# A scan whose two sweeps multiply the state itself instead of its two summands

## The chip, the cores and the metric

One core of a Trainium2 chip runs the whole program. The metric is device time in microseconds (us). The engines are TensorE (PE; its weight loads are listed as PEld), VectorE (DVE), ScalarE (ACT), GpSimd (POOL) and SyncE (SP), which issues most DMAs. Three runs of the kernel before took 1889.16, 1890.15 and 1891.19 us.

## The reference

The input is one sequence of 4096 rows of 512 values, and a context of 3202 rows. All is float32.

```python
x = residual + _mha(layernorm(x), layernorm(ctx), W_qkv, b_qkv, W_o, b_o)   # 8 heads of 64
U = (layernorm(x) @ W_in.T + b_in) @ Bmat                                   # 4096 x 64

def step(s, u_t):
    s = silu(s @ A.T) + u_t
    return (s, s)
_, states = scan(step, zeros(64), U)                                        # 4096 steps in a row
x = x + states @ Cmat + mod
```

The change touches the scan alone: a chain of 4096 steps, each a product with a 64x64 matrix, a silu and an addition.

## The kernel before, in words

**Attention.** The queries are cut into 8 blocks Q of 512, and each block into units (Q, hp, half): a pair of heads hp and half of the block's queries. A unit goes through 13 key chunks; for each, PE makes `s` (L1144), ACT takes the exponential to `p` (L1222), PE makes the product `po` (L1280), and DVE adds `p` up in `acc` (L1230). When a unit is through, PE sums `acc` over the partitions into two banks `pd` (L1309), ACT copies them to `rd` (L1353), DVE takes the reciprocal (L1358), the sum of it (L1361) and scales the unit's output `o` (L1369). The last unit of all, (7, 3, 1), has one tile `pd_last` instead of these banks. For the last 256 queries, the projections `yb` (L2112) take all four head pairs of block 7: `o_7_0_1` holds pairs 0 and 1, `o_7_2_1` pairs 2 and 3.

**The scan.** The 4096 steps are cut into 256 chunks of L = 16 steps. 128 chunks lie in the free dimension and two halves of 64 states in the partitions, so that one step of all chunks is one operation on a 128x128 tile. The tile `u` holds 2U. Sweep "a" (`sweep` at L1971, tiles `za`) starts every chunk at zero. Its last states, `end1`, moved on by one chunk, start sweep "b" (tiles `z`), whose states are the result; the end of b is compared with the end of a, and if anything differs by more than TOL a general and slow path runs. That path doesn't run here.

A step needs z, the product of the matrix with the state. The state is h + u, where h = (1 + tanh(z/2)) z. The kernel before never multiplies the sum. `terms` (L1962) multiplies four steps of `u` at once into a PSUM bank of 4 x 128 columns, ahead of the steps, and `z_` (L1984) adds the product with h to a quarter of that bank. So the chain of a step is: PE `z` (L1960), ACT tanh (L1988), DVE h (L1995), PE `z` again. The state itself is made beside the chain, in sweep b alone, by POOL (L2027, two tiles). `products` (L2034) multiplies it with C into 512 columns for each half. Of its two results, one is added to the row by DVE (L2054); the other, for two steps in three, is copied by ACT (L2048) and added by POOL (L2051), and for the third by DVE. Rows of odd steps have both results in `pd_last`, rows of even steps in `py_n` and `py_o`.

The last 256 rows go through layer norm and a scan of their own (`l.*`: L2133 to L2177, tiles `zl`) with warm-up steps, while sweep b runs.

**Order.** All this is recorded by a planner (`Plan`, L76). Each piece has an engine, a cost, the pieces it waits for, tiles of rings that it takes and gives back, and a due time; `SHIFT` (L94) moves the due time of each sort of piece. An engine takes the ready piece that is due first, and the order that comes out is fixed in the program. Two things matter below. Sweep a takes both tiles of the ring "m" when it opens, and gives them back with its last h; the sums `pd` of a unit need the same two tiles. And `PORT` (L92) names the DVE pieces that the planner keeps apart from POOL's.

The tail also holds dummy products: `idle_` (L2241) multiplies a constant 128x128 tile six times after the last step of b. The comparisons (`largest`, `differ`, L2070 to L2084) take the largest state, times TOL, the difference, its absolute value (on ACT), a comparison of each element and a count.

Of the kernel before, what the change touches and what calls it, by code (L numbers as in the profile page):

```python
# [13 lines left out]
AF = mybir.ActivationFunctionType  # L14
# [6 lines left out]
P = 128  # L21
# [14 lines left out]
WARM = 17  # L36
# [4 lines left out]
NCK = T // L // 2  # L41
NP = 11
# [33 lines left out]
class Plan:  # L76
# [18 lines left out]
        "row.store": 2.25, "fold": 21, "rows.outs": -27.25, "heads": 29.5, "spread": 4.5, "query.flip": -21,  # L95
        "states": 3.25, "inverse": 13.25, "extra": 54.75, "scale": -26, "rest": -11.5, "row.mod": -26.25,
        "joined0": 23.25, "b": -0.75, "add.l": -43.5, "l.stats": -74.25, "last": -0.25, "base": -119.25,
        "inverse.l": 12, "rows.inputs": 7, "maximum": -21, "fall": -14.75, "query.stats": 25, "den": -41.5,
        "row.scaled": -22.75, "l.h": 9.25, "row.stats": -52.75, "rows.turn": 10.25, "query.scaled": -65,
        "l.mod": 24.75, "close": -30, "swap": 32, "products": -9.75, "gather.l": -2.75, "l.ys": 51.5,  # L100
        "fall.l": -46.25, "weights": -14, "rows.s": -6.5, "l.x1": 12.25, "l.kept": 1.5, "tq": 37.5,
        "l.store": 35, "row.move3": -73, "l.from": 2.5, "l.copy": -22.75, "l.states": -42.5, "l.turn": -27.25,
        "row.flip": -51, "swap.l": -30.75, "l.near": -25.75, "differ": 2.25, "row.load": 38, "add": 3.25,
        "rest.l": -23, "den.l": -33, "query.factors": 32, "sevenths": 5, "l.z": -5.75, "scale.l": 64.25,
        "outs": 1.5, "output": -59, "query.move3": 10, "number": -8.75, "l.inputs": -15, "q": -3.75,
        "sums": -35, "row.move2": -22.25, "row.move1": 18.25, "query.move0": 62.75, "stored1": -5.5,
        "counted": -14.25, "to": -30.75, "sums.l": -14.75, "row.kept": 17.75, "so": 19, "stored0": 28.25,
        "l.scaled": 3.5, "row.move0": 0.25, "rise": -31.75, "join": -29.5, "sample": -0.5, "l.idle": -22.75,
        "risen": -59.75, "c2": 7.5, "yb": -16, "query.load": 55.25, "query.move2": 13.75, "row.row": -53.75,
        "added": -31.75, "l.terms": -17.75, "joined1": -4.75, "rows.first": -84.5, "sq": -29.75,  # L110
        "row.x1": 30.75, "join.l": 99.75, "start": 18.5, "sevenths.read": -15.75, "product": 0.5,
        "row.factors": -40, "fold.l": 20, "output.l": 47, "table": -34.75, "gather": 18, "outs.read": -15,
        "copied": 0.5, "open": -6.25, "row.copy": 48.5, "l.out": 31.75, "l.factors": -10.25, "a": 32.5,
        "query.move1": 5.25, "fetch": 19.75, "py1": 22.75,
# [118 lines left out]
def xattn_ssm_kernel(  # L233
# [1663 lines left out]
    A_PACE, B_PACE = 1500, 1900  # L1897
# [33 lines left out]
    def open_scan():  # L1931
# [15 lines left out]
        for name, n in (  # L1947
            ("end0", NCK + 1), ("end1", NCK + 1), ("ul", PRE + 1 + P), ("hw", P), ("hl", P),
            ("sl", P + 1), ("df", NCK), ("st", P // LT),
            ("top", 1), ("bad", 1), ("badl", 1), ("badr", 1),  # L1950
        ):
            sv[name] = two[:, at_ : at_ + n]
            at_ += n
# [8 lines left out]
    def terms(z, q, start):  # L1962

        if q:
            on_a(z, u[:, 4 * q - 1 : 4 * q + 3, :], start=True)
            return
        if start is not None:
            on_a(z[:, 0, :], start, start=True)
        on_a(z[:, 1:, :], u[:, :3, :], start=start is None)

    def sweep(k, start, end, d=0, pace=0, after=()):  # L1971

        def bank(q):
            return sv["za" if k == "a" else "z"][q % 2]

        def at_(j):
            return bank(j // 4)[:, j % 4, :]

        def terms_(q):
            terms(bank(q), q, None if start is None else sv[start][:, :NCK])

        def z_(j):  # L1984
            on_a(at_(j), sv["h"][(j - 1) % 3], start=False)

        def tanh_(j):
            nc.scalar.activation(sv["th"][j % 2], at_(j), AF.Tanh, scale=0.5)  # L1988

        def h_(j):  # L1990
            h = sv["h"][j % 3]
            if j == 0 and start is None:
                nc.vector.memset(h, 0.0)
                return
            nc.vector.scalar_tensor_tensor(  # L1995
                h, sv["th"][j % 2], 1.0, at_(j), ALU.add, ALU.mult
            )

        def last_():
            e = sv[end]  # L2000
            nc.vector.tensor_tensor(e[:, 1:], sv["h"][(L - 1) % 3], u[:, L - 1, :], ALU.add)
            nc.vector.tensor_copy(e[NS:, 0:1], e[:NS, NCK : NCK + 1])

        for j in range(L):
            q = j // 4
            if j % 4 == 0:

                free = [(k, "h", 4 * q - 5)] if q > 1 else list(after)
# [693 lines left out]
```

## Time and profile before

| what | us |
|---|---|
| median of three runs | 1890.15 |
| the profiled execution's own time | 1889.67 |
| its span, first to last instruction | 1887.9 |
| what lies around the span | 1.77 |
| PE busy in it | 1873.1 |
| first product of sweep a | 1782.89 |
| first product of sweep b | 1843.93 |
| last DVE instruction of the main program | 1883.88 |

All times inside the program below are counted from the start of the span. In a timeline row stand the start, the length (from the first start to the last end, where several instructions are drawn together), the engine, the line, the operation, output<-inputs, their number, and in brackets how long the engine was idle before and what ended that. In a row of the groups stand the line, the engine, the operation, the shapes, the number, the busy time in us and the mean of one in ns, and the idle time before them.

### The profile page before, as it was taken

The page shows a single profiled execution, that of the slowest core. Times are in us where ns is not written, and L with a number is a line of the kernel's source. Part 1 is how long each engine was busy: PE and PEld are TensorE (multiplying, and loading weights), DVE is VectorE, ACT ScalarE, POOL GpSimd, SP SyncE. Part 2 cuts the span into 40 slices and gives each one's busy share as a digit, 9 for nine tenths or more (in the row PEclk, how much of TensorE's full clock was granted, in tenths as well). Part 3 has the DMA queues.
Part 4 walks back from the last instruction along what each step waited for, and adds up shares of the span by engine and source line. Part 5 has one row for each costly group of instructions (what it writes and reads, how often), then busy time and mean ns, then how long its engine had stood idle before and what let it go on. Part 6 is the DMA issues. An engine that isn't in the chain of part 4 may idle for free.

```text
span 1887.9 us, 69209 instructions
## 1 busy us (share of the span) xinstructions
PE 1873.1 (99%) x29856; PEld 1414.9 (75%) x29856; DVE 1563.3 (83%) x2142; ACT 1166.6 (62%) x1663; POOL 258.2 (14%) x386
## 2 busy tenths in 40 slices
PE   9999999999999999999999999999999999999997
PEld 5887689777777777797777777777777777777684
DVE  6642699788988889798978898898979897989776
ACT  3242577665766577565756676757757575757653
POOL 6120300022000210022002200021002200110105
PEclk9999999999999999999999999999999999999999
DMA  8554133133323333233313332324313331536477
GB/s 257 158 159 120 54 102 92 38 115 90 106 74 105 86 112 97 65 95 111 98 44 108 87 114 79 106 79 117 98 55 98 107 104 44 171 108 182 139 190 238
DMA packets 260770, 207.58 MB, mean 110 GB/s; under 512 B 94632, under 2 KB 233896, under 8 KB 260460
## 3 DMA queue, kind: packets, MB, share of 16 engines
q1 hardware_dynamic: 256440, 196.48, 36.1%
q10 hardware_dynamic: 4020, 6.62, 1.2%
q8 instruction: 237, 3.88, 0.8%
q14 instruction: 73, 0.60, 0.1%
HBM read 156.32 MB, written 29.88 MB: 99 GB/s over the span
## 4 chain that ended last, share of the span: by engine, by line
PE 97%; DVE 1%; ACT 1%; DMA 0%; issue 0%; POOL 0%; SPq 0%; DVEq 0%; ACTq 0%; POOLq 0%
PE po L1280 37%; PE s L1144 36%; PE pax L404 3%; PE qx L404 3%; PE qy L404 2%; PE pay L404 2%; PE pkx L404 2%; PE pvx L404 2%; PE pvy L404 1%; PE pky L404 1%; PE pk L722 1%; PE pv L599 1%; PE pd L1309 1%; PE sm L1164 1%; PE po L1268 1%; PE pu L1747 1%
## 5 line engine op out<-in xcount | busy, mean ns | idle before, releaser
L1222 ACT ACTIVATE p<-s,shifts 128x1024 f32<-128x1024 f32 (+1 forms) x832 | 891.4, 1081 | 418.3 <-PE s L1144 392.7
L1230 DVE TENSOR_TENSOR acc<-p,acc 128x1024 f32<-128x1024 f32 (+1 forms) x704 | 851.0, 1214 | 96.8 <-ACT p L1222 77.2
L1144 PE MATMUL s<-q,k 64*64 64x256 f32 x12800 | 850.6, 376 | 0.2 <-ACT p L1222 0.2
L1280 PE MATMUL po<-p,v 64*64 64x256 f32 x12800 | 848.2, 376 | 1.0 <-DVE o L1335 0.9
L1144 PEld LDWEIGHTS s<-q,k 64*64 64x64 f32 x12800 | 518.9, 133 | 175.2 <-ACT p L1222 13.5
L1280 PEld LDWEIGHTS po<-p,v 64*64 64x64 f32 x12800 | 519.9, 133 | 163.1 <-issue 3.5
L1634 POOL TENSOR_TENSOR xr<-xr,rowb 128x512 f32<-128x512 f32 x28 | 35.7, 1274 | 797.6 <-DVE acc L1230 688.9
L1358 DVE RECIPROCAL rd<-rd 128x256 f32<-128x256 f32 (+1 forms) x64 | 110.0, 1719 | 6.4 <-ACT rd L1353 6.4
L1249 ACT COPY swap<-acc 64x256 f32<-64x256 f32 x126 | 50.8, 403 | 64.9 <-DVE acc L1237 61.8
L1230 DVE TENSOR_TENSOR acc<-p,p 128x1024 f32<-128x1024 f32 x64 | 78.2, 1222 | 11.6 <-ACT p L1222 11.5
L1729 POOL TENSOR_TENSOR xr<-x,modb 128x512 f32<-128x512 f32 x28 | 41.6, 1496 | 253.3 <-DVE acc L1254 178.3
L1420 POOL TENSOR_SCALAR rstd_x<-mv_x 128x1 f32<-128x1 f32 x28 | 18.6, 666 | 276.7 <-DVE mv_x L1417 276.0
L1215 DVE TENSOR_TENSOR acc<-x,acc 2x256 f32<-2x256 f32 x128 | 54.9, 429 | 1.5
L1254 DVE TENSOR_TENSOR acc<-swap,acc 64x256 f32<-64x256 f32 x126 | 52.4, 416 | 2.9 <-ACT swap L1249 1.3
L1570 ACT ACTIVATE q<-qx,bias 128x256 f32<-128x256 f32 x42 | 17.6, 470 | 48.0 <-PE qx L404 48.0
L582 DVE TENSOR_TENSOR ks<-pky,ks 128x512 f32<-128x512 f32 x15 | 10.4, 692 | 43.2 <-PE pky L404 23.7
L576 ACT ACTIVATE ks<-pkx,bias 128x256 f32<-128x256 f32 x40 | 16.8, 470 | 44.4 <-PE pkx L404 32.9
L1237 DVE TENSOR_TENSOR acc<-acc 128x512 f32<-128x512 f32 x63 | 43.1, 684 | 0.3
L1335 DVE TENSOR_TENSOR o<-po,o 128x256 f32<-128x256 f32 x64 | 27.0, 423 | 14.1 <-ACT o L1331 13.5
L481 DVE STREAM_TRANSPOSE x<-xh_y 128x512 f32<-128x512 f32 x28 | 18.2, 688 | 21.7 <-ACT xh_y L1428 14.7
L1353 ACT ACTIVATE rd<-pd 128x128 f32<-128x128 f32 x126 | 34.0, 275 | 1.0 <-PE pd L1309 0.4
L1178 DVE TENSOR_REDUCE m<-sm 128x1 f32<-128x256 f32 x64 | 24.0, 417 | 11.3 <-PE sm L1164 11.3
(314 smaller groups left out, 1760.7 us busy)
## 6 DMA issues: line engine op xcount, KB each, us to landing
k<-kd SPq DMA_DIRECT2D x432, 128.0 KB, 2.2
v<-vd SPq DMA_DIRECT2D x432, 128.0 KB, 2.2
xn<-x SPq DMA_DIRECT2D x448, 32.0 KB, 1.9
xr<-in_x_dram SPq DMA_DIRECT2D x30, 256.0 KB, 3.2
x1d<-xr SPq DMA_DIRECT2D x30, 256.0 KB, 2.2
x<-in_x_dram SPq DMA_DIRECT2D x28, 256.0 KB, 3.0
cx<-in_ctx_dram SPq DMA_DIRECT2D x25, 256.0 KB, 4.2
kd<-ks SPq DMA_DIRECT2D x20, 256.0 KB, 2.3
```

The costliest lines, as they stand in the source:

```text
L404: nc.tensor.matmul(to[:, b, :], still[:, i, b * P : (b + 1) * P], moving[:, i, :], start=(start and b == 0 and i == 0), stop=(i == 1), ski ...
L1144: nc.tensor.matmul(s[k0 : k0 + HD, a, b, :], kts[(*w["at"][:2], c)][r, b * CK + k0 : b * CK + k0 + HD], q[r], start=True, stop=True, skip_ ...
L1215: made = nc.vector.tensor_tensor(to[r], t[r], to[r], ALU.add)
L1222: nc.scalar.activation(t[:, :, :nb, :], w["ps"][c][:, :, :nb, :], AF.Exp, bias=w["shift"])
L1230: return nc.vector.tensor_tensor(w["acc"][:, :, :nb, :], t[:, :, :nb, :], before[:, :, :nb, :], ALU.add)
L1237: return nc.vector.tensor_tensor(acc[:, :, 0, :], acc[:, :, 0, :], acc[:, :, 1, :], ALU.add)
L1249: nc.scalar.copy(w["swap"][r], of[(1 - k) * HD : (2 - k) * HD])
L1254: made = nc.vector.tensor_tensor(of[r], w["swap"][r], of[r], ALU.add)
L1280: nc.tensor.matmul(w["po"][k][a * HD : (a + 1) * HD, :QU], vts[Q, hp, c][r, b, a * HD : (a + 1) * HD], t[r, a, b, :], start=(c == 0 and b ...
L1358: nc.vector.reciprocal(w["rd"][:, part], (w["pd"] if last else w["rd"])[:, part])
L1634: return nc.gpsimd.tensor_tensor(xs[half][:, t], xs[half][:, t], rowb, ALU.add)
L1729: return nc.gpsimd.tensor_tensor(xt[:, t], x1[:, t], modb, ALU.add)
```

## The change

1. `terms` is gone. Both sweeps make h as before, then DVE adds `u` to it (a new piece "s", L1980 of the changed kernel) into one of five tiles (NST), and `z_` multiplies that state. PE's sixteen products of `u` (eight in each sweep) go; DVE gets 15 additions in sweep a and 16 in sweep b, less the one in `last_` of each sweep, which becomes a copy.
2. POOL's sixteen additions of sweep b go, since the state is there already. The new piece is not in `PORT`.
3. The six dummy products go.
4. A comparison is now one DVE piece: largest state times TOL, difference, largest absolute difference, comparison of one column. ACT's Abs goes.
5. B_PACE goes from 1900 to 1600, and nearly every number of `SHIFT` is another.

```diff
-WARM = 17
+NST = 5
...
-        "row.store": 2.25, "fold": 21, "rows.outs": -27.25, "heads": 29.5, "spread": 4.5, "query.flip": -21,
+        "row.store": -5.25, "fold": 15.25, "rows.outs": 0.25, "heads": 5, "spread": 4, "query.flip": 3.75,
...
-    A_PACE, B_PACE = 1500, 1900
+    A_PACE, B_PACE = 1500, 1600
...
-        sv["th"] = [one[:, i, :] for i in range(2)]
-        sv["h"] = [one[:, 2 + i, :] for i in range(3)]
-        sv["s"] = [one[:, 5 + i, :] for i in range(2)]
-        sv["ok"] = one[:, 7, :]
+        sv["th"], sv["h"], sv["ok"] = (one[:, i, :] for i in range(3))
+        sv["s"] = [one[:, 3 + i, :] for i in range(NST)]
...
-    def terms(z, q, start):
-
-        if q:
-            on_a(z, u[:, 4 * q - 1 : 4 * q + 3, :], start=True)
-            return
-        if start is not None:
-            on_a(z[:, 0, :], start, start=True)
-        on_a(z[:, 1:, :], u[:, :3, :], start=start is None)
...
+        def state(j):
+            if j < 0:
+                return sv[start][:, :NCK]
+            return sv["s"][j % NST] if j or start is not None else u[:, 0, :]
 
         def z_(j):
-            on_a(at_(j), sv["h"][(j - 1) % 3], start=False)
+            on_a(at_(j), state(j - 1), start=True)
...
+        def state_(j):
+            nc.vector.tensor_tensor(state(j), sv["h"], u[:, j, :], ALU.add)
 
         def last_():
             e = sv[end]
-            nc.vector.tensor_tensor(e[:, 1:], sv["h"][(L - 1) % 3], u[:, L - 1, :], ALU.add)
+            nc.vector.tensor_copy(e[:, 1:], state(L - 1))
...
+        first = 1 if start is None else 0
+        for j in range(first, L):
+            free = [(k, "s", j - 1)] if j > first else list(after)
+            yield (k, "z", j), "PE", 250, partial(z_, j), free, d, [], [], "quarters"
+            yield (k, "tanh", j), "ACT", 240, partial(tanh_, j), [(k, "z", j)], d + 400
+            gives = [("m", "open")] if k == "a" and j == L - 1 else []
+            yield (k, "h", j), "DVE", 210, partial(h_, j), [(k, "tanh", j)], d + 800, [], gives
+            old = [("products", j - NST, part) for part in range(2)] if first == 0 and j >= NST else []
+            yield (k, "s", j), "DVE", 210, partial(state_, j), [(k, "h", j)] + old, d + 800
             d += pace
-        yield (k, "end"), "DVE", 450, last_, [(k, "h", L - 1)], d
-
-    def states(j, h):
-        s = sv["s"][j % 2]
-        nc.gpsimd.tensor_tensor(s, h, u[:, j, :], ALU.add)
-        return s
+        yield (k, "end"), "DVE", 350, last_, [(k, "s", L - 1)], d
...
         nc.vector.tensor_tensor(df, new, old, ALU.subtract)
-        yield
-        nc.scalar.activation(df, df, AF.Abs)
-        yield
-        nc.vector.tensor_scalar(ok, df, top, None, ALU.is_le)
-        nc.vector.tensor_reduce(bad, ok, AX.X, ALU.add)
+        nc.vector.tensor_reduce(far, df, AX.X, ALU.max, apply_absolute_value=True)
+        nc.vector.tensor_tensor(bad, far, top, ALU.is_le)
...
-        def idle_():
-            for k in range(2):
-                nc.tensor.matmul(sv["z"][1][:, k, :], a_t, a_t, start=True, stop=True)
...
-            plan.add(("states", j), "POOL", 450, lambda j=j: states(j, sv["h"][j % 3]),
-                     [("b", "h", j)] + ([("products", j - 2, part) for part in range(2)] if j > 1 else []), e)
```

What the planner makes of it. Up to the middle of unit (7, 0, 1), PE's rows are the same one by one. Further on they differ at three places that the prediction speaks of.

PE, from the last attention products on, before. The rows are the last two products of unit (7, 3, 1), its sums `pd_last`, the projections `yb`, and the start of sweep b (`z`).

```order
L1280 MATMUL po0_7_3_1_24264<-p_7_3_1_12_24439,v_7_3_1_12_24251 64x256
L1280 MATMUL po1_7_3_1_24265<-p_7_3_1_12_24439,v_7_3_1_12_24251 64x256
L1296 MATMUL pd_last_24534<-acc_7_3_1_24175,ones_70 64x256 x4
L2112 MATMUL yb_0_24450<-wo_97,o_7_0_1_23457 128x512
L2112 MATMUL yb_1_24451<-wo_97,o_7_0_1_23457 128x512
L2112 MATMUL yb_0_24450<-wo_97,o_7_0_1_23457 128x512
L2112 MATMUL yb_1_24451<-wo_97,o_7_0_1_23457 128x512
L2112 MATMUL yb_0_24450<-wo_97,o_7_2_1_24229 128x512 x2
L2112 MATMUL yb_1_24451<-wo_97,o_7_2_1_24229 128x512 x2
L1960 MATMUL z_24522<-scan_21420,a_t_91 64x128 x2
L1960 MATMUL z_24522<-u_63,a_t_91 64x384 x2
L1960 MATMUL z_24522<-u_63,a_t_91 64x512 x2
```

The same place now, from the fifteenth and last product of sweep a (`za_1`) on, which stands right behind the last product of unit (7, 3, 1); `pd_7_1_1` and `pd_7_2_1` are the sums of the two units before the last.

```order
L1958 MATMUL za_1_23801<-scan_21420,a_t_91 64x128 x2
L1309 MATMUL pd_7_1_1_0_24525<-acc_7_1_1_23367,ones_70 64x128
L1309 MATMUL pd_7_1_1_1_24526<-acc_7_1_1_23367,ones_70 64x128
L1309 MATMUL pd_7_1_1_0_24525<-acc_7_1_1_23367,ones_70 64x128
L1309 MATMUL pd_7_1_1_1_24526<-acc_7_1_1_23367,ones_70 64x128
L1958 MATMUL z_24420<-scan_21420,a_t_91 64x128 x2
L1309 MATMUL pd_7_2_1_0_24541<-acc_7_2_1_23808,ones_70 64x128
L1309 MATMUL pd_7_2_1_1_24542<-acc_7_2_1_23808,ones_70 64x128
L1309 MATMUL pd_7_2_1_0_24541<-acc_7_2_1_23808,ones_70 64x128
L1309 MATMUL pd_7_2_1_1_24542<-acc_7_2_1_23808,ones_70 64x128
L2078 MATMUL yb_0_24551<-wo_97,o_7_0_1_23463 128x512
L2078 MATMUL yb_1_24552<-wo_97,o_7_0_1_23463 128x512
```

Sweep a now ends behind the attention's products; before, its last `z` stood ahead of `s` of chunk 7 of this unit, with six more `s` and the `po` of ten chunks still to come; so the sums that need its two tiles came behind it too, and the first product of sweep b came between them, ahead of the projections. The row that follows is the second `z`, and two more `yb` pairs come behind it.

DVE at the same place, before: reciprocals and scalings of units (7, 2, 1) and (7, 3, 1). Those of unit (7, 1, 1) stand further ahead, between additions to `acc`.

```order
L1358 RECIPROCAL rd_7_2_1_24427<-rd_7_2_1_24427 128x128
L1369 TENSOR_TENSOR o_7_2_1_24229<-o_7_2_1_24229,rd_7_2_1_24427 128x128
L1361 TENSOR_REDUCE rises_90<-rd_7_2_1_24427 128x1
L1369 TENSOR_TENSOR o_7_2_1_24229<-o_7_2_1_24229,rd_7_2_1_24427 128x128
L1335 TENSOR_TENSOR o_7_2_1_24229<-po1_7_3_1_24265,o_7_2_1_24229 128x256
L1358 RECIPROCAL rd_7_3_1_24542<-pd_last_24534 128x128 x2
L1361 TENSOR_REDUCE rises_90<-rd_7_3_1_24542 128x1
L1364 MEMSET rises_90 128x1
L1365 TENSOR_REDUCE rises_90<-pd_last_24534 128x1
L1369 TENSOR_TENSOR o_7_2_1_24229<-o_7_2_1_24229,rd_7_3_1_24542 128x128 x2
```

The same place now, from the last state of sweep a (written as `scan<-scan,u`) on; `scan<-scan,z` is h of sweep b.

```order
L1980 TENSOR_TENSOR scan_21420<-scan_21420,u_63 128x128
L1984 COPY scan_21420<-scan_21420 128x128
L1985 COPY scan_21420<-scan_21420 64x1
L1369 TENSOR_TENSOR o_7_2_1_24207<-o_7_2_1_24207,rd_7_3_1_24497 128x128 x2
L1358 RECIPROCAL rd_7_1_1_24533<-rd_7_1_1_24533 128x256
L1977 SCALAR_TENSOR_TENSOR scan_21420<-scan_21420,z_24420 128x128
L1358 RECIPROCAL rd_7_2_1_24548<-rd_7_2_1_24548 128x128
L1369 TENSOR_TENSOR o_7_0_1_23463<-o_7_0_1_23463,rd_7_1_1_24533 128x256
L1361 TENSOR_REDUCE rises_90<-rd_7_1_1_24533 128x1
L1980 TENSOR_TENSOR scan_21420<-scan_21420,u_63 128x128
L1358 RECIPROCAL rd_7_2_1_24548<-rd_7_2_1_24548 128x128
L1369 TENSOR_TENSOR o_7_2_1_24207<-o_7_2_1_24207,rd_7_2_1_24548 128x128
```

Three reciprocals and two scalings now stand between the end of sweep a and the second state of sweep b, and the steps of sweep b are queued among them.

DVE in sweep b, before, from the h of step 6 on; `row_4` and the like are the results of `products`, added to the rows.

```order
L1995 SCALAR_TENSOR_TENSOR scan_21420<-scan_21420,z_24522 128x128
L2054 SCALAR_TENSOR_TENSOR row_4_24477<-py_n_24588,row_4_24477 128x512
L1995 SCALAR_TENSOR_TENSOR scan_21420<-scan_21420,z_24522 128x128
L2054 SCALAR_TENSOR_TENSOR row_5_24480<-pd_last_24534,row_5_24480 112x512
L2054 SCALAR_TENSOR_TENSOR row_5_24480<-pd_last_24534,row_5_24480 128x512
L1995 SCALAR_TENSOR_TENSOR scan_21420<-scan_21420,z_24522 128x128
L2054 SCALAR_TENSOR_TENSOR row_6_24483<-py_n_24588,row_6_24483 128x512
```

The same place now, from the h of step 8 on.

```order
L1977 SCALAR_TENSOR_TENSOR scan_21420<-scan_21420,z_24420 128x128
L1980 TENSOR_TENSOR scan_21420<-scan_21420,u_63 128x128
L2023 SCALAR_TENSOR_TENSOR row_5_24446<-pd_last_24472,row_5_24446 112x512
L2023 SCALAR_TENSOR_TENSOR row_5_24446<-pd_last_24472,row_5_24446 128x512
L1977 SCALAR_TENSOR_TENSOR scan_21420<-scan_21420,z_24420 128x128
L2023 SCALAR_TENSOR_TENSOR row_6_24449<-py_n_24609,row_6_24449 128x512
L1980 TENSOR_TENSOR scan_21420<-scan_21420,u_63 128x128
L2023 SCALAR_TENSOR_TENSOR row_7_24452<-pd_last_24472,row_7_24452 128x512
L1977 SCALAR_TENSOR_TENSOR scan_21420<-scan_21420,z_24420 128x128
```

Each step has a second DVE instruction behind h, and here and there a row's addition stands between the two.

More of the change, by code (lines that the diff above doesn't have):

```diff
@@ L100 @@
[L100 to L114, printed above, removed]
+        "row.store": -5.25, "fold": 15.25, "rows.outs": 0.25, "heads": 5, "spread": 4, "query.flip": 3.75,
@@ new lines @@
+        "states": 3.25, "inverse": -23.25, "extra": 112.5, "scale": -54.25, "rest": -22.5, "row.mod": -59.25,
+        "joined0": 54.25, "b": -7, "add.l": -20.75, "l.stats": -76.75, "last": -3.75, "base": -103.25,
+        "inverse.l": 22.75, "rows.inputs": -20.75, "maximum": -16.75, "fall": -22.25, "query.stats": 45,
+        "den": -24, "row.scaled": -19, "l.h": 16, "row.stats": -20.25, "rows.turn": 11.5,
+        "query.scaled": -52.75, "l.mod": 82.75, "close": -22.75, "swap": 52.5, "products": -14.25,
@@ L115 @@
+        "l.factors": 66, "a": -11.75, "query.move1": -22.75, "fetch": 3.25, "py1": 47.75, "scores": 0.25,
     }
```

82 lines of the change are left out of this document (26 added, 56 removed), and 3 rows, old and new, of the table SHIFT.

## The prediction, made before the changed kernel ran

> **What bounds the kernel now.** I read the page first, then busy time by stretches, then the lines of the scan, then the timeline around the end of the attention and in the tail.
>
> ```profile
> span 1887.9 us, 69209 instructions
> PE 1873.1 (99%) x29856; PEld 1414.9 (75%) x29856; DVE 1563.3 (83%) x2142; ACT 1166.6 (62%) x1663; POOL 258.2 (14%) x386
> ```
>
> The first number of each engine is its busy time. PE is the bound of the whole. By stretches (PE, PEld, DVE, ACT, POOL, then the granted clock):
>
> ```profile
> 200.00:1842.00 1642.00, 1640.33 (x28453) 1243.03 (x28452) 1437.45 (x1884) 1082.26 (x1488) 179.88 (x240) 1.00 0.35 99
> 1800.00:1840.00 40.00, 39.64 (x662) 32.82 (x655) 33.82 (x50) 23.94 (x41) 3.67 (x2) 1.00 0.76 196
> 1842.00:1880.00 38.00, 34.82 (x477) 21.49 (x475) 25.31 (x59) 14.93 (x51) 23.15 (x30) 1.00 0.76 240
> 1874.34:1884.00 9.66, 5.74 (x70) 3.44 (x66) 8.79 (x22) 2.45 (x9) 4.65 (x5) 0.99 0.93 311
> ```
>
> Up to 1842 PE stands still for 1.7 us of 1642, so a product removed there is time gained. From 1842 to 1880 it is busy 34.82 of 38, and the chain of the scan begins to count. In the last ten microseconds DVE is busy 8.79 of 9.66 and sets the end. So the change has three stages with three different bounds. Up to unit (7, 0, 1) nothing that PE does has moved, and I take no difference there.
>
> **Sweep a's products of u.**
>
> ```profile
> L1960 PE MATMUL za<-u,a_t x16: 482/589/589, 1782.9 to 1804.9; 64*64 64x512 f32 x12, 64*64 64x384 f32 x4
> L1960 PE MATMUL z<-u,a_t x16: 481/589/640, 1844.2 to 1863.2; 64*64 64x512 f32 x12, 64*64 64x384 f32 x4
> ...
> 1782.89 1.68 PE L1960 MATMUL za<-u,a_t 64*64 64x384 f32 x8
> 1784.39 0.27 PE L1960 MATMUL za<-scan,a_t 64*64 64x128 f32 x1
> ```
>
> Eight records of the first bank (384 columns, then 512) hold PE from 1782.89 to 1784.39: 1.50 us for 896 columns, 1.67 ns a column. (Each product of the program is two records, and the two halves run side by side.) A sweep has 384 + 3 x 512 = 1920 columns, so **3.2 us** go from each. Sweep a's go in full. By the same price one product with a state, 128 columns, is 0.21 us.
>
> **From the attention's end to the projections' end.** Sweep a now ends later, and its last waits fall on PE:
>
> ```profile
> 1823.07 0.28 DVE L1995 SCALAR_TENSOR_TENSOR scan<-scan,za 128x128 f32<-128x128 f32 x1
> 1823.38 0.29 DVE L2001 TENSOR_TENSOR scan<-scan,u 128x128 f32<-128x128 f32 x1
> ...
> 1825.03 1.75 DVE L1358 RECIPROCAL rd<-rd 128x256 f32<-128x256 f32 x1
> 1827.77 0.41 DVE L1369 TENSOR_TENSOR o<-o,rd 128x256 f32<-128x256 f32 x1
> 1829.23 0.41 DVE L1361 TENSOR_REDUCE rises<-rd 128x1 f32<-128x256 f32 x1
> 1829.59 0.41 PE L1309 MATMUL pd<-acc,ones 64*64 64x128 f32 x5
> 1832.24 0.95 DVE L1358 RECIPROCAL rd<-rd 128x128 f32<-128x128 f32 x1
> 1843.93 0.44 PE L1960 MATMUL z<-scan,a_t 64*64 64x128 f32 x4
> ```
>
> Before, the last scores of unit (7, 3, 1) end at 1829.59, where the sums of (7, 2, 1) begin, and the first product of sweep b starts 14.34 us later. Now four products of sweep a and the sums of (7, 1, 1) (about 0.2) move behind this point, so it comes at 1829.6 - 3.2 - 5 x 0.21 = 1825.3. From it PE has the same 14.34, and 7 x 0.21 = 1.5 more: four products of a, the first two of b and the moved sums. And it waits. By the orders quoted above, the last product of a waits for a state that stands on DVE among two reciprocals (0.9 each) and a reduction: **1.4**. The first of b waits for tanh, h, the last state and the two copies: **1.4**. The second waits for the reciprocal of (7, 1, 1), one of (7, 2, 1), a scaling, a reduction and its own addition, 1.75 + 0.95 + 0.41 + 0.41 + 0.3 = 3.8, less the sums and four projections that PE makes meanwhile: **2.1**. Together 4.9, an estimate. The projections end at 1825.3 + 14.3 + 1.5 + 4.9 = **1846.0** against 1843.9: the 3.2 us gained is lost again, and 2.1 more. In return, two steps of b are made.
>
> **Sweep b.** A step of it in the middle, alone, and the sweep's last product:
>
> ```profile
> 1864.24 0.33 PE L1960 MATMUL z<-scan,a_t 64*64 64x128 f32 x2 [0.37 <-DVE scan L1995]
> 1864.73 0.28 ACT L1988 ACTIVATE scan<-z 128x128 f32<-128x128 f32 x1 [0.58 <-PE z L1960]
> 1865.11 0.29 DVE L1995 SCALAR_TENSOR_TENSOR scan<-scan,z 128x128 f32<-128x128 f32 x1 [0.32 <-ACT scan L1988]
> 1865.50 0.39 PE L1960 MATMUL z<-scan,a_t 64*64 64x128 f32 x4
> ...
> 1874.34 0.27 PE L1960 MATMUL z<-scan,a_t 64*64 64x128 f32 x1
> ```
>
> The chain alone takes 1865.50 - 1864.24 = 1.26. The 15 steps take 1874.34 - 1843.93 = 30.4, or 2.03 each; the rest is products, rows and the scan of the last rows in between. Of this, 3.2 / 15 = 0.21 are products of u, and go. The addition comes into the chain: 0.31, the distance of h and addition in sweep a (1823.07 to 1823.38). And that addition may have to wait for POOL:
>
> ```profile
> 1876.47 1.26 POOL L2051 TENSOR_TENSOR row<-y_l,row 112x512 f32<-112x512 f32 x1
> 1876.53 1.36 DVE L2001 TENSOR_TENSOR scan<-scan,u 128x128 f32<-128x128 f32 x1
> ...
> L2079 DVE TENSOR_TENSOR scan<-scan 128x128 f32<-128x128 f32 x1 | 0.3, 282 | 0.0
> L1995 DVE SCALAR_TENSOR_TENSOR scan<-scan,z 128x128 f32<-128x128 f32 x16 | 4.6, 286 | 7.9 <-ACT scan L1988 6.2 <-PE zl L1960 1.2 <-POOL scan L2027 0.4
> L2051 POOL TENSOR_TENSOR row<-y_l,row 112x512 f32<-112x512 f32 x8 | 10.3, 1282 | 3.2 <-ACT y_l L2048 3.2
> ```
>
> The addition of the last state starts 0.06 us after POOL's addition of a row and ends with it: 1357 ns, where the same shape (L2079) takes 282. h itself, which reads z, has a mean of 286 over 16 with POOL busy. So h never waits, and the new addition does, if POOL began first. POOL's additions cover 10.3 us of the 21 from 1855 to 1876, 49%; a start at random would wait 0.49 x 0.64 = 0.31. Addition and POOL's row hang on the same chain and need not meet at random; bounds are 0 and one whole row's addition for each of some nine, 8.7 x 1.28 = 11.1 us. I take 0.25 a step, near the random value. A step is 2.03 - 0.21 + 0.31 + 0.25 = 2.38, and the thirteen left take 30.9: the last product comes at 1846.0 + 30.9 = **1876.9, 2.6 later**. The sixteen additions that leave POOL (L2027) lay beside the chain, and I count nothing for them.
>
> The Trainium skill, "SBUF — State Buffer", section "Who interferes with whom", says that a DVE instruction with two SBUF inputs contends with a GpSimd instruction that reads SBUF, and that the later one is blocked for the whole of the earlier. The row of 1357 ns agrees. By that rule alone, without a say on the order, the step would lie anywhere between 2.13 and 2.13 plus a row's addition.
>
> **The end.**
>
> ```profile
> 1875.96 1.60 PE L2241 MATMUL z<-a_t 128*128 128x128 f32 x12
> 1879.02 0.15 DVE L2074 TENSOR_SCALAR scan<-scan 128x1 f32<-128x1 f32 x1
> 1879.88 0.28 DVE L2083 TENSOR_SCALAR scan<-scan 128x128 f32<-128x128 f32 x1
> 1882.02 1.13 DVE L2083 TENSOR_SCALAR scan<-scan 128x32 f32<-128x32 f32 x1
> 1883.88 0.14 DVE L2440 TENSOR_SCALAR nbad<-pd_last 1x1 int32<-1x1 f32 x1
> ```
>
> From the last product to the last DVE instruction are 9.5 us, nearly all DVE. The comparison of elements goes (0.28, and about 0.2 for the small one), a comparison of one column comes (0.15 each): -0.2. The small one took 1.13 beside a row's addition on POOL, about 0.9 of it waiting: -0.9 if nothing waits in its place. Of the 1.08 that the last addition waited I take a third to go. Abs ran beside DVE's addition of a row, and counts nothing. The dummies go, for which the last step's products waited; DVE has rows to add meanwhile, so nothing. Sum **-1.5**, bounds -2.2 and -0.2.
>
> **The sum.** 2.6 - 1.5 = +1.1 on the profiled execution: its own time 1889.67 (span 1887.9 and 1.77 around it) becomes **1890.8**. The median of the three runs shown is 1890.15, 0.48 above the profiled one. A measurement of this kernel can tell about 0.2%, 3.8 us, from no change, that is 1886.4 to 1893.9: the forecast is no change that can be measured.
>
> **The rivals.**
>
> *Faster: all that leaves PE comes out.* 3.2 and 3.2 from the sweeps and 1.5 at the end give 1889.7 - 7.9 = **1881.8**. For it speaks PE's 99%; against it, that the queue on DVE at the end of sweep a is read off the order. It needs the 4.9 us of waits to vanish. If only POOL's additions fall so that none is met, it is 13 x 0.25 less, **1887.6**.
>
> *Slower: the state's addition is locked out by POOL in sweep b.* The row reaches POOL through products, ACT's copy and a queue; if its addition begins just ahead of the next state in most steps, nine steps bear 1.28 each, 11.1 instead of 3.2: **1898.7**. It decides the sign from about half of these steps on (6.9 us in all), 1894.5. For it: the one addition with `u` that meets a row's addition in the tail was blocked in full.
>
> *Slower: additions to `acc` hold up sweep a.*
>
> ```profile
> 1821.05 2.10 DVE L1230 TENSOR_TENSOR acc<-p,acc 128x1024 f32<-128x1024 f32 x1
> 1819.80 2.27 POOL L2349 TENSOR_TENSOR xr_l<-xr_l,rowb 128x512 f32<-128x512 f32 x1
> ```
>
> DVE is busy 33.8 of 40 us from 1800 to 1840; an addition to `acc` takes 1.2, and one beside POOL took 2.10. A product of sweep a whose state stands behind such a one stops PE. Five of them at 1.2 make 6: **1897**. Against it: between two products of a stand whole groups of attention products.
>
> *The clock.*
>
> ```profile
> 1883.00:1884.00 1.00, 0.24 (x4) 0.14 (x4) 0.96 (x4) 0.00 (x0) 0.11 (x1) 0.86 0.79 297
> 1884.00:1888.00 4.00, 0.00 (x0) 0.00 (x0) 0.02 (x1) 0.00 (x0) 0.00 (x0) 0.50 0.40 137
> ```
>
> Some 4 us after PE's last stretch of work, the granted clock falls to 0.86 and then 0.50. Without dummies, and with waits among sweep b's first steps, PE could fall to this inside the work; at half the clock six microseconds of products would take six more: **1897**. The longest wait I forecast is 2.1, so this is unlikely. The Trainium skill, "TensorE: Matmul & The Clock Gate", section "Part 1: The HAM clock gate (the "warmup" mystery)", has the clock halved after an idle window of about 3.4 us; the fall behind the last work agrees, and no idle stretch of that length is forecast. By the rule the sum stays.
>
> *The change doesn't do what it says:* no; the order has sixteen products of u and six dummies fewer, and nothing in their place.
>
> **How the numbers follow.** My forecast, no measurable change: 0.46. Faster 0.23, of which 0.1 lies at the full gain of PE's work. Slower 0.31: POOL's lock 0.18, `acc` 0.07, the clock 0.03, other waits 0.03. The bounds of the lock are 1887.6 and 1898.7, and the end adds 1 at either side. The range reaches from **1883.5**, halfway into the first rival, to **1898.7**, and leaves out about 0.08 on each side.
>
> **What would show it.** First product of sweep b ahead of the projections, and these ending at about 1846; PE waiting 5 us between the attention's last scores and that point; 2.4 us a step in sweep b; a mean of the new addition (L1980) near 530 ns there, 280 if no lock is met and over 900 for the slower rival; the last DVE instruction 8.0 us after the last product. The forecast is wrong if PE waits under 2 us at the end of sweep a, if L1980's mean in the tail leaves 350 to 750 ns, or if PE's clock falls below 1.00 before the last product.

## The result, and the profile after

The changed kernel takes 1895.93 us (median of nine, 1894.70 to 1898.06) against 1889.57 before: a ratio of 1.0034, 95% interval 1.0025 to 1.0043. It is slower by 0.34%. The forecast was 1890.8, no change that can be measured. The range (1883.5 to 1898.7) held; "no change" did not, for 1895.93 lies above the 1893.9 that the prediction had set as its limit. The profiled execution took 1898.06, the slowest of the nine; the sums below go by it, and the sizes of causes by medians.

The page's first lines, then three stretches: from the scores of unit (7, 3, 1)'s last full key chunk to the end of the projections, on to the last product of sweep b, on to the end (busy time of PE, PEld, DVE, ACT, POOL, then the granted clock).

```profile
span 1896.3 us, 69094 instructions
PE 1872.2 (99%) x29812; PEld 1401.6 (74%) x29812; DVE 1576.0 (83%) x2172; ACT 1168.1 (62%) x1661; POOL 250.5 (13%) x370
...
1825.54:1846.87 21.33, 18.80 (x170) 9.48 (x163) 15.24 (x36) 6.47 (x19) 0.00 (x0) 0.92 0.97 231
1846.87:1883.02 36.15, 28.62 (x390) 18.90 (x389) 27.97 (x58) 12.48 (x41) 15.10 (x13) 0.86 0.54 185
1883.02:1892.55 9.53, 4.38 (x54) 2.11 (x54) 8.38 (x23) 2.32 (x8) 2.53 (x2) 0.98 0.55 186
```

The work on PE is less, and the clock in the last rows is not 1.00. The rows that set these borders:

```profile
1824.35 1.19 PE L1144 MATMUL s<-q,k 64*64 64x256 f32 x16
1837.64 3.58 PE L2078 MATMUL yb<-wo,o 128*128 128x512 f32 x4 [0.46 <-ACT rd L1353]
1846.87 0.33 PE L1958 MATMUL z<-scan,a_t 64*64 64x128 f32 x2
1883.02 0.33 PE L1958 MATMUL z<-scan,a_t 64*64 64x128 f32 x2 [0.17 <-DVE scan L1980]
1892.41 0.14 DVE L2391 TENSOR_SCALAR nbad<-pd_last 1x1 int32<-1x1 f32 x1
```

What the prediction calls the last scores are those of the last full chunk; before and after, eight products for the rest of the keys follow (at 1827.45 here). The scores end at 1825.54 (forecast 1825.3), the projections at 1846.87 (1846.0), the last product stands at 1883.02 (1876.9), the last DVE instruction 9.39 behind it (8.0). Most of the loss lies in sweep b. What happens there, from its longest step on:

```profile
1848.92 1.27 POOL L2020 TENSOR_TENSOR row<-y_l,row 112x512 f32<-112x512 f32 x1 [1.14 <-ACT y_l L2017]
1850.09 3.21 DVE L1980 TENSOR_TENSOR scan<-scan,u 128x128 f32<-128x128 f32 x1
1850.14 0.55 POOL L2107 TENSOR_TENSOR rstd_yl<-rstd_yl,neg_half 128x1 f32<-128x1 f32 x1
1850.66 2.48 POOL L2141 TENSOR_TENSOR xr_l<-x_l,modb 128x512 f32<-128x512 f32 x2
1853.35 0.69 PE L1958 MATMUL z<-scan,a_t 64*64 64x128 f32 x4 [3.67 <-DVE scan L1980]
1853.97 1.97 PE L2127 MATMUL pu_l<-xn_l,wc 128*64 128x128 f32 x8
...
1852.00:1858.00 6.00, 4.65 (x28) 3.30 (x28) 2.88 (x7) 1.14 (x3) 1.14 (x1) 0.50 0.32 115
```

The addition of u takes 3.21 us: it starts 0.1 before POOL's addition of a row ends, and ends 0.16 behind POOL's two additions of the modulation to the last 256 rows. PE waits 3.67. The clock falls to 0.50 at 1851.1, during this wait, and stays there until 1858.0, so that PE's next 4.6 us of work run at half clock: eight products of the last rows' inputs take 1.97, where they take 1.09 at full clock (e1, in the next section). The groups of sweep b, with the mean in ns, and what PE waited for from 1815 on (us in all, times, longest):

```profile
L1980 DVE TENSOR_TENSOR scan<-scan,u 128x128 f32<-128x128 f32 x16 | 11.1, 695 | 0.3
L1977 DVE SCALAR_TENSOR_TENSOR scan<-scan,z 128x128 f32<-128x128 f32 x15 | 4.3, 284 | 6.1 <-ACT scan L1974 5.9
...
PE z L1958 <- DVE scan L1980: 6.1, 6, 3.7
PE za L1958 <- DVE scan L1980: 1.6, 3, 0.7
```

h, which reads z in PSUM, never waits for POOL (284); the addition has a mean of 695 where 282 to 290 is its length alone, 6.6 us of waiting in sixteen. 2.9 of it is the one beside the modulation, 3.7 is beside additions of rows (3.0 ahead of the last product, 0.7 in the last step).

### The profile page after: what moved, and what is told of

It reads as the page before. It is cut to its first block, busy times and chain, and to the rows that moved or that the text cites. A ratio compares the mean times of both kernels' runs of the same rounds, so it can differ in the third digit from the quotient of the medians.

```text
span 1896.3 us, 69094 instructions
## 1 busy us (share of the span) xinstructions
PE 1872.2 (99%) x29812; PEld 1401.6 (74%) x29812; DVE 1576.0 (83%) x2172; ACT 1168.1 (62%) x1661; POOL 250.5 (13%) x370
## 4 chain that ended last, share of the span: by engine, by line
## 5 line engine op out<-in xcount | busy, mean ns | idle before, releaser
L1144 PEld LDWEIGHTS s<-q,k 64*64 64x64 f32 x12800 | 513.2, 133 | 180.7 <-ACT p L1222 13.4
L1280 PEld LDWEIGHTS po<-p,v 64*64 64x64 f32 x12800 | 512.2, 133 | 169.9 <-issue 3.9
```

The costliest lines, as they stand in the source:

```text
L1144: nc.tensor.matmul(s[k0 : k0 + HD, a, b, :], kts[(*w["at"][:2], c)][r, b * CK + k0 : b * CK + k0 + HD], q[r], start=True, stop=True, skip_ ...
L1280: nc.tensor.matmul(w["po"][k][a * HD : (a + 1) * HD, :QU], vts[Q, hp, c][r, b, a * HD : (a + 1) * HD], t[r, a, b, :], start=(c == 0 and b ...
```

## The experiments

**Theory L:** POOL locks out the state's addition, and what hangs on it. **Rival D:** the place of sweep a's end in the order. **Rival C:** the clock that falls where PE waits. **Rival S:** a second DVE step on the chain, whatever it waits for. Five rounds each; each with the kernel before on the same chip:

| run | us | before | ratio, 95% interval |
|---|---|---|---|
| the change | 1895.93 | 1889.57 | 1.0034, 1.0025 to 1.0043 |
| e1_psum_state | 1890.53 | 1889.06 | 1.0007, 0.9998 to 1.0016 |
| e2_no_mod | 1891.96 | 1889.06 | 1.0015, 1.0006 to 1.0024 |
| e3_warm | 1899.34 | 1889.06 | 1.0055, 1.0041 to 1.0068 |
| e4_no_terms | 1887.75 | 1889.06 | 0.9996, 0.9987 to 1.0005 |
| e8_end_only | 1891.86 | 1889.13 | 1.0016, 1.0007 to 1.0025 |
| e10_sweep_b_only | 1895.05 | 1889.13 | 1.0031, 1.0020 to 1.0043 |
| e11_sweep_b_psum | 1891.88 | 1889.13 | 1.0015, 1.0006 to 1.0024 |
| e12_sweep_b_psum_end | 1890.69 | 1889.13 | 1.0009, 0.9999 to 1.0018 |
| e13_psum_late_mod | 1888.28 | 1889.05 | 0.9995, 0.9986 to 1.0004 |
| e14_late_mod_warm | 1887.50 | 1889.05 | 0.9991, 0.9982 to 1.0000 |
| e15_warm_z3 | 1895.01 | 1889.15 | 1.0032, 1.0019 to 1.0044 |
| e16_last_row | 1886.95 | 1889.15 | 0.9988, 0.9979 to 0.9997 |

**e1: the lock taken away, in the same order.** h is written back over z, so the addition has one input in SBUF.

```diff
-            nc.vector.scalar_tensor_tensor(sv["h"], sv["th"], 1.0, at_(j), ALU.add, ALU.mult)
+            nc.vector.scalar_tensor_tensor(at_(j), sv["th"], 1.0, at_(j), ALU.add, ALU.mult)
-            nc.vector.tensor_tensor(state(j), sv["h"], u[:, j, :], ALU.add)
+            nc.vector.tensor_tensor(state(j), at_(j), u[:, j, :], ALU.add)
```

> The changed kernel, in the same order, with h written back into its quarter of z in PSUM, so that the addition of u has one input in SBUF instead of two. Theory L (the additions of sweep b wait while POOL reads SBUF): no addition of the state above 0.35 us in the tail; the waits of 2.9 and 0.3 to 1.0 us seen after the change, 6.6 us in all, go, and the half clock that followed the longest with them: 1886 to 1890 us. Rival D (the waits for reciprocals at the end of sweep a are the loss): not above 2 us gained, 1894 or more. Rival S (a second DVE step on the chain is the loss, whatever it waits for): 1893 or more.

1890.53, 5.4 us less than the change by medians (5.1 by the ratios to before): theory L, if a little over its range. The groups of sweep b, then the place where the lock went:

```profile
L1980 DVE TENSOR_TENSOR scan<-z,u 128x128 f32<-128x128 f32 x16 | 4.6, 286 | 0.3
...
1849.37 2.49 POOL L2141 TENSOR_TENSOR xr_l<-x_l,modb 128x512 f32<-128x512 f32 x2
1849.44 2.70 DVE L2111 TENSOR_SCALAR xh_yl<-x_l,mv_yl,rstd_yl 128x512 f32<-128x512 f32 x1 [0.37 <-POOL rstd_yl L2107]
1849.49 1.09 PE L2127 MATMUL pu_l<-xn_l,wc 128*64 128x128 f32 x8
1852.20 0.66 PE L2117 MATMUL py_o<-ident,xh_yl 128*128 128x128 f32 x4 [1.62 <-DVE xh_yl L2111]
```

All sixteen additions take 286. But the modulation now holds up the normalisation of the last rows, 2.70 us in place of 0.55, and PE waits for that.

**e2: without the modulation.**

```diff
         def mod_(g):
-            nc.gpsimd.tensor_tensor(xl[g], v["x1"][g], modb, ALU.add)
+            pass
```

> The changed kernel, in the same order, without POOL's two additions of the modulation to the last 256 rows (L2141): this part of the output is left out. Theory L: the addition of 3.2 us falls to 0.3 and z of the next step comes 2.9 us earlier; the half clock after that wait goes as well and gives about 2 us more: 1890 to 1893 us. If waits on POOL are covered by something else that is late next: within 1 us of the changed kernel, 1895 to 1897. Rival D: no change.

1891.96: 3.6 (by the ratios) to 4.0 us (by medians) of the loss hang on two POOL instructions that the change itself didn't touch. The same addition of u, in the same place between POOL's row and its factor, now takes 0.28:

```profile
1850.24 1.27 POOL L2020 TENSOR_TENSOR row<-y_l,row 112x512 f32<-112x512 f32 x1 [1.14 <-ACT y_l L2017]
1851.41 0.28 DVE L1980 TENSOR_TENSOR scan<-scan,u 128x128 f32<-128x128 f32 x1
1851.47 0.62 POOL L2107 TENSOR_TENSOR rstd_yl<-rstd_yl,neg_half 128x1 f32<-128x1 f32 x1
```

**e3: dummy products where PE waits.**

```diff
+    def warm(n):
+        for _ in range(n):
+            nc.tensor.matmul(sv["z"][1][:, 3, :], a_t, a_t, start=True, stop=True)
...
         def z_(j):
+            warm({("a", 15): 3, ("b", 1): 3, ("b", 3): 10}.get((k, j), 0))
...
+        if c == 0 and tiles == [0]:
+            warm(3)
```

> The changed kernel, in the same order, with dummy products in PE's queue where it was seen to wait: 3 ahead of the last z of sweep a, 3 ahead of the first yb, 3 ahead of z 1 and 10 ahead of z 3 of sweep b. Theory C (after such waits TensorE runs at half clock, and this is a large part of the loss): granted clock 1.00 from 1836 to 1842 and from 1852 to 1858, where the changed kernel showed 0.5 to 0.87; yb about 1 us shorter, the products behind z 3 about 2 us shorter: 1892 to 1893.5 us. Theory L alone: the clock is of no account, and the dummies cost nothing or up to 1 us: 1895.5 to 1897.

1899.34, 3.4 more, and against both. The run doesn't answer its question, for two reasons. The dummies ahead of the projections waited 1.5 us for a read of the tile they write, and the projections behind them ended 1 us later. And from the last DVE instruction to the end of the span were 6.9 us, where the change has 3.9 (see the last section). The clock did stay at 1.00 from 1836 to 1860.

**e4: the products of u alone.** In the kernel before, `terms` issues only the first product with the start, and each product with h starts its quarter.

```diff
-        if q:
-            on_a(z, u[:, 4 * q - 1 : 4 * q + 3, :], start=True)
-            return
-        if start is not None:
+        if not q and start is not None:
             on_a(z[:, 0, :], start, start=True)
-        on_a(z[:, 1:, :], u[:, :3, :], start=start is None)
...
-            on_a(at_(j), sv["h"][(j - 1) % 3], start=False)
+            on_a(at_(j), sv["h"][(j - 1) % 3], start=True)
```

> The kernel before, in the same order, without the sixteen products of u (the scan then computes other states; TOL is so large that the slow path doesn't run). It measures what the removed products were worth by themselves. By the prediction 3.2 us in sweep a, and up to 3.2 in sweep b: 1883.2 to 1886.5 us. Rival: sweep b is bound by its chain, so only sweep a's come out: 1886 to 1887. If PE's products of u lay in gaps: 1889 or more.

1887.75, by medians 1.3 us for 6.4 us of products, outside all three ranges; the interval (0.9987 to 1.0005) doesn't tell it from nothing. In its profile (of the longest of its runs, 4.2 us above the median) the sums of (7, 2, 1) come at 1828.68, 0.9 earlier than before and not 3.2, and later PE stands still for something that the profile doesn't show:

```profile
1782.50:1829.60 47.10, 44.98 (x824) 37.24 (x821) 38.44 (x55) 31.45 (x49) 3.58 (x2) 1.00 0.61 164
...
1836.26 0.43 PE L1280 MATMUL po<-p,v 64*64 64x256 f32 x1 [1.73 <-issue]
```

PE waits 2.1 of these 47 us, 1.3 of it for h of sweep a (before, 0.5 and 0.3). So even at 99% busy not every removed product is time gained: part of it becomes waiting for what stands behind it.

**e8: the end alone.** Parts 3 and 4 of the change in the kernel before; its diff is that of the change.

> The kernel before with parts 3 and 4 of the change alone: no dummy products, and the comparisons by the largest difference. The prediction gave -1.5 us for the end, 1887.5 to 1888. Rival, after the changed kernel's trace, where a waiting subtraction took the place of the comparison that waited for POOL: no change, 1888.7 to 1889.5.

1891.86: 2.7 slower, outside both. From its last product of b (1874.13) to its last DVE instruction (1884.26) are 10.1 us, where 9.5 were before, and to the end of the span 7.1 more in place of 4.0, as in e3. These last 3.1 us are no work of the end (see the last section), so the run's time doesn't price the end; its rows do: nothing is gained on DVE, and the wait has moved on:

```profile
1878.71 1.26 POOL L2051 TENSOR_TENSOR row<-y_l,row 112x512 f32<-112x512 f32 x1 [1.19 <-DMA out_dram<-row]
1878.87 1.25 DVE L2079 TENSOR_TENSOR scan<-scan 128x128 f32<-128x128 f32 x1
```

The last products end 0.7 us earlier than before (1877.9), and ACT copies their result 3.1 earlier (1878.04 in place of 1881.17, where it stood behind Abs). So POOL's last row meets the subtraction, which took 0.28 before.

**e10, e11, e12: sweep b alone.** Sweep a as before, sweep b as in the change, in the order numbers of before; e11 with h in PSUM, e12 with the end of e8 as well.

```diff
+        direct = k != "a"
...
         def z_(j):
-            on_a(at_(j), sv["h"][(j - 1) % 3], start=False)
+            if direct:
+                on_a(at_(j), state(j - 1), start=True)
+            else:
+                on_a(at_(j), sv["h"][(j - 1) % 3], start=False)
...
+        def state_(j):
+            nc.vector.tensor_tensor(state(j), sv["h"][0], u[:, j, :], ALU.add)
```

(e11: `at_(j)` in place of `sv["h"][0]`, here and as the result of h, and five state tiles in place of four.)

> The kernel before with part 1 of the change in sweep b alone (four state tiles, the addition of u on DVE from two inputs in SBUF, POOL's sixteen additions gone); sweep a keeps its products of u and its place in the order. Theory L: the additions of the state wait for POOL again, some above 1 us, and more than the 3.2 us of products saved is lost: 1891 to 1895. Theory D (sweep a's place in the order is the loss): 1886 to 1889.

> The same as the run with sweep b alone, with h written back into z's quarter in PSUM (five state tiles). Against it this shows the lock alone: 3 to 6 us faster. Against the kernel before it shows what 3.2 us of products less in sweep b are worth against one more step on the chain: 1886 to 1889.5 us; 1887 if half of them come out.

> The sum of the runs e8_end_only and e11_sweep_b_psum: 1885 to 1889 us. It may beat both the kernel before and the changed one; if the sweep's gain lies before an end that DVE sets, the two gains don't add, and it equals the better of them.

1895.05, 1891.88, 1890.69. e10 speaks for L and against D: sweep a keeps its place, and nearly the whole loss is there. The additions of e10, then of e11:

```profile
L1996 DVE TENSOR_TENSOR scan<-scan,u 128x128 f32<-128x128 f32 x16 | 9.0, 560 | 0.4
```

```profile
L1996 DVE TENSOR_TENSOR scan<-z,u 128x128 f32<-128x128 f32 x16 | 4.6, 287 | 0.4
```

The lock is worth 3.2 us here, if the fifth state tile is worth nothing. e11 missed its range by 2.4 and e12 by 1.7: without this lock, sweep b's form is still slower than before (e11; e12's interval takes in 1) in an order that was not made for it.

**e13: the modulation later.** e1, with POOL's two additions behind the last rows' inputs.

```diff
-            plan.add(("l.mod", g), "POOL", 1250, partial(mod_, g), [("l.x1", g), ("l.factors", 1)],
+            plan.add(("l.mod", g), "POOL", 1250, partial(mod_, g), [("l.x1", g), ("l.kept", 1)],
```

> The run e1_psum_state with one more edit: POOL's two additions of the modulation come behind the last rows' inputs (one row's addition later in POOL's order). In e1 they no longer held the state's addition but the normalisation of the last rows (L2111: 2.70 us in place of 0.55), and PE waited 1.6 us for it, with half clock behind. Theory L (what POOL blocks decides): L2111 at 0.55 us, that wait gone, the half clock from 1854 to 1858 with it: 2 to 4 us less than e1, 1886.5 to 1888.5 us, below the kernel before. Rival (the last rows are not on the path): within 0.7 us of e1.

1888.28, 2.25 less than e1, as L has it; L2111 is back at 0.55. Sweep b's third and last product:

```profile
1847.35 0.33 PE L1958 MATMUL z<-scan,a_t 64*64 64x128 f32 x2
...
1874.85 0.33 PE L1958 MATMUL z<-scan,a_t 64*64 64x128 f32 x2
```

27.5 us for thirteen steps are 2.12 each, and 2.03 - 0.21 + 0.31 = 2.13 was the prediction's step without a lock. So the second step on the chain costs about what the row said, 0.1 us a step more than before: against S as the cause.

**e14: dummies that wait for nothing.**

```diff
+    def warm(n, to):
+        for _ in range(n):
+            nc.tensor.matmul(to, a_t, a_t, start=True, stop=True)
...
     def sums(w):
+        if w["at"] == (NQB - 1, 1, 1):
+            warm(4, sv["z"][1][:, 3, :])
...
+            if (k, j) == ("a", 15):
+                warm(3, sv["z"][1][:, 3, :])
+            if (k, j) == ("b", 1):
+                warm(3, sv["pd"][:, 1, :P])
...
+        if c == 0 and tiles == [0]:
+            warm(2, sv["pd"][:, 1, :P])
```

> The run e13_psum_late_mod with twelve dummy products where PE waits at the end of sweep a, in PSUM that nothing reads there (unlike e3_warm, whose dummies waited for a read): 3 ahead of the last z of sweep a, 4 ahead of the sums of (7, 1, 1), 2 ahead of the first yb, 3 ahead of z 1 of sweep b. Theory C: granted clock 1.00 from 1834 to 1842 (e1: 0.50 to 0.67 for 4 us), the first four yb in 1.8 us instead of 3.4, z 1 then waits for its state: 0.7 to 1.7 us less than e13. Without an effect of the clock: the same time as e13, or up to 0.7 more.

1887.50, 0.8 less than e13. The stretch and the first projections of e13, then of e14:

```profile
1836.00:1842.00 6.00, 5.54 (x16) 2.12 (x16) 5.13 (x11) 0.90 (x5) 0.00 (x0) 0.50 1.05 282
...
1837.01 3.78 PE L2078 MATMUL yb<-wo,o 128*128 128x512 f32 x4 [0.46 <-ACT rd L1353]
```

```profile
1836.00:1842.00 6.00, 5.85 (x30) 3.48 (x31) 5.62 (x13) 1.35 (x9) 0.00 (x0) 1.00 1.06 257
...
1837.26 1.97 PE L2091 MATMUL yb<-wo,o 128*128 128x512 f32 x4
```

The clock is 1.00 and not 0.50, and the four projections take half the time. By medians, twelve products without a use make the kernel faster; the two intervals overlap, and the rows agree with C.

**e15: one fall priced in the changed kernel.**

```diff
         def z_(j):
+            if (k, j) == ("b", 3):
+                for _ in range(12):
+                    nc.tensor.matmul(at_(j), a_t, a_t, start=True, stop=True)
```

> The changed kernel, in the same order, with twelve dummy products ahead of z 3 of sweep b alone, where PE waits 3.7 us for the state that POOL holds up. It prices one fall of the clock inside the changed kernel. Theory C: clock 1.00 from 1853 to 1858, z 4 about 1.5 to 2.5 us earlier than without: 1893.3 to 1894.5 us. Theory L alone (the lock's wait is the price, the clock only looks bad): 1895.5 to 1897.

1895.01, 0.4 (by the ratios) to 0.9 us (by medians) less than the change: between the two ranges, and the intervals don't tell it from nothing. The two steps behind the long wait, in this run and after the change:

```profile
1852.86 0.44 PE L1958 MATMUL z<-scan,a_t 64*64 64x128 f32 x4 [0.80 <-DVE scan L1983]
1854.83 0.33 PE L1958 MATMUL z<-scan,a_t 64*64 64x128 f32 x2
```

```profile
1853.35 0.69 PE L1958 MATMUL z<-scan,a_t 64*64 64x128 f32 x4 [3.67 <-DVE scan L1980]
...
1856.91 0.48 PE L1958 MATMUL z<-scan,a_t 64*64 64x128 f32 x2
```

1.97 in place of 3.56: 1.6 us in these profiles for this fall, less over all runs. This fall is a small part of the price, and follows the lock.

**e16: nothing left for POOL at the end.** e14, with the last row added by DVE.

```diff
-        spread = j % 3 < 2
+        spread = j % 3 < 2 and j < L - 1
```

> The run e14_late_mod_warm with the last row's second result added by DVE, so that POOL has nothing left when the ends are compared. In e1 the subtraction of the comparison took 1.35 us beside POOL's last row. Theory L: it takes 0.3; DVE has one addition of 0.69 more; 0.4 us less than e14, up to 1 less. Rival (the wait moves on to another place, as it did from the comparison to the subtraction in e8): the same as e14, or 0.7 more.

1886.95, 0.55 less than e14 and 0.12% below the kernel before (0.9988, 0.9979 to 0.9997): the one version whose interval lies below 1. The subtraction in e14, then here:

```profile
1877.72 1.35 DVE L2059 TENSOR_TENSOR scan<-scan 128x128 f32<-128x128 f32 x1
```

```profile
1877.72 0.28 DVE L2059 TENSOR_TENSOR scan<-scan 128x128 f32<-128x128 f32 x1
```

By medians, then: 5.4 us for the lock on the state with what follows from it, 2.25 for the lock on the last rows, 0.8 for the clock behind sweep a, 0.55 for the lock at the end: 9.0 between the change and e16 (8.7 by the ratios). For the last three of these the intervals of the two runs compared overlap.

## Why the prediction was right in its range and wrong in its centre

- **No difference up to the last units; sweep a's products come out.** Right: the scores end at 1825.54, 0.2 from the forecast. e4 shows that this was not bound to be so. The rival of additions to `acc` that hold up sweep a stayed small: PE waited 1.6 us for states of a (row `za` above).
- **From the attention's end to the projections' end.** 21.3 us against 20.7. The sum came out by luck: PE waited 2.5 us and not 4.9 (21.33 - 18.80), and was busy 3.0 longer than the 15.8 I had, some 1.6 of it from the half clock (3.2 us of work at 0.50). Of the waits, the last product of a had 0.7 of its 1.4, the first of b 0.1; 0.8 ahead of a `po`, for which the profile names no cause, and two of 0.5 were not forecast. The second product of b did not wait 2.1 for its state; the four projections ahead of it took 3.58 at half clock and covered the wait.
- **Sweep b, the step that failed.** 36.15 us for thirteen steps against 30.9. The step without a lock was right (2.12 in e13, 2.13 forecast), and so was the lock of POOL's rows: 3.0 us ahead of the last product, 3.2 forecast. L1980's mean of 695 lies in the band that the prediction gave itself; without the addition of 3.21 the other fifteen have 527, where 530 was forecast. Wrong was that I counted POOL's rows alone. POOL's other instructions of the tail, the two additions of the modulation, were left out; before, they ran beside h, which doesn't wait. One addition met them and bore 2.9 us (e2: worth 3.6 to 4.0 with what followed). The other 2.5 us of the miss fit the half clock, at which PE worked 8.0 us of this stretch, but no run prices all of that.
- **The clock, put at 0.03 as a rival.** I held it to need an idle stretch of some 4 us, and named a clock below 1.00 ahead of the last product as a mark of being wrong. It fell to 0.5 three times ahead of the last product: at 1837.5 and 1878.4 behind waits of at most 1.1 each, and at 1851.1, 1.4 us into the wait of 3.7. The first fall is there without a lock too (e1, e13); in e13 the other two are gone. So at these two lock and clock were not separate cases: the one brought the other on.
- **The end, -1.5.** Measured -0.15 (9.39 against 9.54). "If nothing waits in its place" was the condition, and something did: in place of the comparison the subtraction waited for POOL's last row.

```profile
1887.88 1.26 POOL L2020 TENSOR_TENSOR row<-y_l,row 112x512 f32<-112x512 f32 x1 [2.22 <-ACT y_l L2017]
1887.95 1.34 DVE L2048 TENSOR_TENSOR scan<-scan 128x128 f32<-128x128 f32 x1
```

In sum 0.9 + 5.2 + 1.4 = 7.5 is, to 0.2, the 7.3 by which the profiled execution was off (1898.06 against 1890.8); by the median it was 5.1.

The rule of the Trainium skill, "SBUF — State Buffer", section "Who interferes with whom", that the prediction named (the later of two such instructions is blocked until the earlier is through) agrees with these traces where POOL's instruction is an addition of 512 columns: each addition of u with a length above 0.35 us ended 0.1 to 0.2 behind such a one, and with h in PSUM none of sixteen waited (e1). It doesn't show beside POOL's factor of 128x1: in e10 an addition took 0.29 (1847.42) within the 0.55 of such a factor, though POOL's spans are rough.

What stays open: why e11 is 2.8 us slower than before without a lock, and how much of the change's remaining loss in e1 is the order and how much the chain.

## What to carry to other kernels

An operation that moves from POOL to DVE with both inputs in SBUF has to be weighed against every POOL instruction that can run at that time, not only against those of its own loop; write one operand to PSUM, as e1 writes h over z, and it need not wait: none of the sixteen did. A lock that is taken away shows up at the next such instruction, so follow the list of POOL's instructions to the end of the program. And a wait of PE on a short chain is paid a second time if the clock falls with it.

## What was not expected of the hardware

The granted clock falls without an idle stretch of microseconds, and it falls on a grid. Followed in stretches of 0.5 us after the change, it falls to 0.50 at 1837.47, 1851.12 and 1878.43: 13.65 and 27.31 us apart, 4 and 8 times 3.41. The half clocks last one, two and one such window. The windows in which it fell at the end, and what followed:

```profile
1834.06:1837.47 3.41, 2.11 (x24) 1.31 (x24) 3.09 (x11) 1.57 (x9) 0.00 (x0) 1.00 1.06 247
1837.47:1840.88 3.41, 3.24 (x4) 1.18 (x4) 3.41 (x7) 0.38 (x4) 0.00 (x0) 0.50 1.06 251
...
1847.71:1851.12 3.41, 1.70 (x22) 0.63 (x12) 3.29 (x8) 1.19 (x2) 2.27 (x4) 1.00 0.02 6
1851.12:1854.53 3.41, 1.18 (x7) 0.85 (x8) 2.76 (x3) 0.28 (x1) 2.02 (x2) 0.50 0.77 274
...
1875.02:1878.43 3.41, 1.82 (x36) 1.32 (x34) 2.48 (x4) 1.65 (x6) 2.50 (x2) 1.00 0.97 343
1878.43:1881.84 3.41, 3.41 (x40) 2.69 (x39) 2.22 (x6) 1.25 (x5) 0.30 (x1) 0.50 0.56 180
```

PE was busy 62%, 50% and 53% of the windows ahead of the falls. In e1, e2, e4, e10, e13 and e15 too each half clock ahead of the last product lasts 3.4 or 6.8 us, and PE was busy 42% to 68% of the window ahead; no window above 70% was followed by a fall, and between 59% and 68% there are windows of both kinds. So by these runs it matters how much waiting falls into such a window, and not the longest wait alone. The Trainium skill, "TensorE: Matmul & The Clock Gate", section "Part 1: The HAM clock gate (the "warmup" mystery)", has the half clock after an idle window of about 3.4 us; the length agrees with these rows, but no window here was idle. Further on, the section tells of a kernel whose frequent short idle times sent the clock to and fro; the rows are of this second kind.

In e3 and e8 6.9 and 7.1 us lie between the last DVE instruction and the end of the span, in the other runs 3.6 to 4.0. No engine has an instruction there, but the waits of SP's queue (e3, then e8) differ:

```profile
SPq L2657 <- PEq L2573: 2.3, 1, 2.3
SPq L2686 <- PEq L2602: 3.0, 1, 3.0
```

SP waits for PE's sequencer at the branch behind the main program (`tc.If`), which it does in no other run, and two instruction transfers on queue q8 fall into this stretch, where the others have one. Why PE's sequencer came late wasn't tested.
